# Weight folds on ScalarE, and a new pair's first chunk ahead of the last conv chunk

## The chip, the core and the metric

The kernel runs on one core of a Trainium2 chip. Its metric is the time of one execution in microseconds (us). The core's engines work through their own instruction queues, each in the order in which the program was written: TensorE (PE, matrix products), VectorE (DVE), ScalarE (ACT, activation functions), GpSimd (POOL) and SyncE (SP, which here issues the loads and stores). They meet through semaphores.

## What is computed

The input is 16 images of 192 channels and 56x56 positions in float32. Three layers of a bidirectional RWKV recurrence are followed by a graph convolution. Each has a group normalization in front and adds its result to its input. Cut to what matters:

```
def layer(x):                                  # three times
    xs = tokens(group_norm(x))                 # 3136 tokens of 192 channels
    k, v, r = xs @ Wk.T, xs @ Wv.T, xs @ Wr.T
    w = -exp(w_decay)
    x_bi = 0.5 * (wkv_scan(w, u, k, v) + flip(wkv_scan(w, u, flip(k), flip(v))))
    h = layer_norm(sigmoid(r) * x_bi)
    return x + (h @ Wo.T)

def conv(x):                                   # once, at the end
    g = group_norm(x)
    m = max(roll(g, 2, H), roll(g, -2, H), roll(g, 2, W), roll(g, -2, W)) - g
    y = batch_norm(conv_w @ concat(g, max(m, 0)) + conv_b)
    return x + gelu(y)
```

`wkv_scan` is a weighted running average over the tokens: a numerator p and a denominator q decay by the factor exp(w) per token, and the current token enters with a bonus exp(u).

## The kernel before

Two images form a pair, so that 2 x 192 channels fill three groups of 128 partitions. There are 8 pairs. The 3136 tokens are cut into 7 chunks of 448. A forward unit of a layer, called A, does one chunk in rising order: the key product (`a_keys`) and its exponential (`a_exp`), the value product (`a_values`), exp(k) times v (`a_ekv`), the scans of q and p (`a_q`, `a_p`, line 850), the bonus on each (`a_den`, `a_num`, line 865), the inverse of q as exp(-ln q) on ACT (`invert`), and the quotient on POOL (`a_y`). The scan's last column is copied into the next chunk's tile: `a_save` (ACT) for q, and line 861 within `a_p` for p. A backward unit, B, does one chunk in falling order: the gate product (`b_gate`, `b_exp`, `b_sigmoid`), the scans and bonuses (`b_q`, `b_p`, `b_den`, `b_num`), `b_mix` on POOL (nine operations, lines 991 to 993), and then a tail in stages: squares (ACT) and sums (PE), `b_rs1` to `b_rs3` for the deviation, `b_spread` (PE, tile `rsb`) and `b_scale` (DVE), `b_out` (PE), and `b_x` (DVE, called by `add`), which adds to x. `sum_up` calls `b_stats`, which counts sums and sums of squares of the new x on ACT (lines 724 and 725, tile `fjunk`). A conv unit, C, does two products per chunk (`c_product`), the maxima (`c_rows`, `c_columns`, lines 1075 to 1091, on DVE), and `c_end` with Gelu on ACT and an addition on POOL (L1118). `z_stats` counts the statistics of a later pair's input, one chunk (Z) at a time, on ACT, at the end of a step.

The normalization isn't applied to x: `norm_sums`, `norm_var` and `norm_fold` turn the statistics into a factor per channel, refine it by one Newton step (lines 765 to 768), and multiply the weights of keys and values by it (`fold`, lines 758 to 760, tile `wkv`). For the conv layer line 771 first subtracts one half of the weights from the other. `norm_fold_r` does the gate weights on POOL. These four parts stand in a list, and each call of `gap()` executes one; `begin_now` executes what is left when a unit needs its weights.

The order of all work is written out by hand. A list of 249 steps is made first; a step holds at most one B unit of one pair and one A or C unit of another. There are two streams, the even and the odd pairs, and while one stream runs a layer backwards the other runs its next layer forwards. Each step is executed by one function:

- `both_a` and `both_a_first` (102 steps): B beside A. 25.0 us in the middle of a layer.
- `both_c` (42 steps): B beside C. About 24 us.
- `backward_alone` (24 steps): the first B chunk of a layer.
- `forward_a` and `forward_c` (66 and 14 steps): a lone chunk.
- `neither` (one step): `finish` does what is left of the tails.

At six places a new pair starts: step 53 has the last backward chunk of the other stream beside C5, step 54 is the lone conv chunk C6, and steps 55 to 61 are the seven chunks of the new pair's first layer, A0 to A6, all alone. The other five places are at steps 69, 116, 131, 178 and 193. At the program's start the first pair's A0 to A6 are alone as well (steps 0 to 6), and at its end the last pair's seven conv chunks (steps 242 to 248). The dictionary `late` holds the tails that aren't done, by stage: 0 (nothing yet), 0.5 (`b_rs1` done), 1 (deviation done), 2 (product done, to be added). In `forward_a` and `forward_c` the tail's parts stand between the parts of the chunk, and the parts for the next chunk's keys (`keys`, `exp_keys`) too.

Loads are issued on SP by `load_ahead`, stores by `store` and `b_x`; tiles come from a list of 33 slots and 7 PSUM banks.

Of the kernel before, what the change touches and what calls it, by code (L numbers as in the profile page):

```python
# [40 lines left out]
C = 192  # L41
# [432 lines left out]
def fast_path(ctx: ExitStack, tc: tile.TileContext, flag, x, wproj, wfold, wcfold, wconst, wgroup, sums, picks, vecs, out):  # L474
# [280 lines left out]
        V.tensor_copy(s.full[:, :, L : L + 1], run.nm)  # L755

    def fold(eng, w, rstd):
        eng.tensor_scalar(w[:, :, 0:C], w[:, :, 0:C], rstd[:, 0, :], None, ALU.mult)
        eng.tensor_scalar(w[:, :, C : 2 * C], w[:, :, C : 2 * C], rstd[:, 2, :], None, ALU.mult)
        eng.tensor_scalar(w[:, :, 2 * C : FCOLS], w[:, :, 2 * C : FCOLS], rstd[:, 1, :], None, ALU.mult)  # L760

    def norm_fold(run):
        rstd, t = run.rstd, stile("gt")

        V.tensor_mul(t, rstd, rstd)
        V.tensor_mul(t, t, run.var)
        V.tensor_scalar(t, t, -0.5, 1.5, ALU.mult, ALU.add)
        V.tensor_mul(rstd, rstd, t)
        w, wr = run.weights
        if run.l == NLAYERS:  # L770
            V.tensor_sub(w[:, 0, :], w[:, 0, :], w[:, 1, :])
        fold(V, w, rstd)
        run.w = [folded(w[:, 0, :]), folded(w[:, 1, :])]
        if run.l < NLAYERS:
            run.new = new_stats()
        run.begun = True
# [20 lines left out]
        load_ahead(("C" if run.l == NLAYERS else "A", run, 0))  # L797
        norms.extend((part, run) for part in (norm_sums, norm_var, norm_fold, norm_fold_r))

    def gap():  # L800
        if norms:
            part, run = norms.pop(0)
            part(run)

    def begin_now(run):
        while not run.begun:
# [358 lines left out]
    while ready[turn] is not None:  # L1165
        run, other = ready[turn], 1 - turn
        units = []
        ready[other] = None
        while todo[other]:
            r = todo[other].pop(0)  # L1170
            units += front(r)
            if r.l < NLAYERS:
                ready[other] = r
                break
        steps.append([("B", run, NL - 1), None, None])
        for c in reversed(range(NL - 1)):
            steps.append([("B", run, c), units.pop(0) if units else None, None])
        steps += [[None, u, None] for u in units]
        if len(streams) == 1 or ready[other] is None:

            units = []
            while todo[turn]:
                r = todo[turn].pop(0)
                units += front(r)
                if r.l < NLAYERS:
                    ready[turn] = r
                    break
            else:
# [18 lines left out]
    def of_stage(n):  # L1207
        return next((u for u, stage in late.items() if stage == n), None)

    def sum_up():  # L1210
        while unsummed:
            b_stats(*unsummed.pop(0))

    def squares_and_sums(u):
        b_squares(*u)
        b_sums(*u)
# [32 lines left out]
    def both_a(b, a, nback, nfront):  # L1249

        den = lambda: a[0].den[a[1]]
        l = of_stage(0.5)
        load_ahead(nback)
        load_ahead(nfront)
        store()
        if nback is not None:
            b_gate(*nback[1:])
            b_exp(*nback[1:])
        b_q(*b)
        if l:  # L1260
            b_rs2(*l)
            b_rs3(*l)
        b_sigmoid(*b)
        a_values(*a)
        if l:
            b_spread(*l)
        b_p(*b)
        b_den(*b)
        invert(b[0].ek[b[1]])
        b_num(*b)  # L1270
        b_mix(*b)
        if l:
# [12 lines left out]
        b_squares(*b, (2,))  # L1285
        exp_keys(nfront, (1,))
        b_squares(*b, (1,))
        b_sums(*b)
        a_p(*a)
        gap()  # L1290
        a_den(*a)
        b_rs1(*b)
        late[b] = 0.5
        invert(den())
        gap()
        a_num(*a)
        a_y(*a)
        gap()
# [45 lines left out]
    def both_c(b, a, nback, nfront):  # L1344

        l0, l1, l2 = of_stage(0), of_stage(1), of_stage(2)
        load_ahead(nback)
        load_ahead(nfront)
        store()
        b_q(*b)  # L1350
        b_p(*b)
        if l0:
            squares_and_sums(l0)
        b_den(*b)
        ln(b[0].ek[b[1]])
        if l0:
            b_rs1(*l0)
        exp_minus(b[0].ek[b[1]])
        if l2:
            add(l2)  # L1360
            sum_up()
        if l1:
            spread_and_scale(l1)
        gap()
        if nback is not None:
            b_gate(*nback[1:])
            b_exp(*nback[1:])
        c_product(*a, 0)
        c_rows(*a)
        c_columns(*a)  # L1370
        c_product(*a, 1)
        gap()
        if l0:
            b_rs2(*l0)
            b_rs3(*l0)
            late[l0] = 1
        gap()
        b_num(*b)
        b_sigmoid(*b)
        b_mix(*b)  # L1380
        if l1:
            add(l1)
            sum_up()
        if nback is not None:
            b_q(*nback[1:])
            b_p(*nback[1:])
        if l0:
            spread_and_scale(l0)
        c_end(*a, False)
        keys(nfront)  # L1390
        exp_keys(nfront)
        late[b] = 0

    def forward_a(a, nback, nfront):
        l = next(iter(late), None)
        den = lambda: a[0].den[a[1]]
        a_values(*a)
        load_ahead(nback)
        ahead = nfront is not None and nfront[1].begun
        if ahead:  # L1400
            load_ahead(nfront)
        if l and late[l] == 2:
            add(l)
            l = None
        if l and late[l] == 0:
            squares_and_sums(l)
            b_rs1(*l)
            late[l] = 0.5
        if not l and ahead:
            keys(nfront)  # L1410
        store()
        a_q(*a)
        a_save(*a)
        if l:
            if late[l] == 0.5:
                b_rs2(*l)
                b_rs3(*l)
            b_spread(*l)
            a_den(*a)
            invert(den())  # L1420
            sum_up()
            a_ekv(*a)
            b_scale(*l)
            b_out(*l)
            if nback is not None:
                b_gate(*nback[1:])
            if ahead:
                keys(nfront)
                exp_keys(nfront)
            a_p(*a)  # L1430
            a_num(*a)
            add(l)
            sum_up()
            gap()
        else:
            if ahead:
                exp_keys(nfront)
            a_den(*a)
            gap()
            invert(den())  # L1440
            a_ekv(*a)
            gap()
            sum_up()
            if nback is not None:
                b_gate(*nback[1:])
            a_p(*a)
            gap()
            a_num(*a)
        a_y(*a)
        if nback is not None:  # L1450
            b_exp(*nback[1:])
        if not ahead:
            load_ahead(nfront)
            keys(nfront)
            exp_keys(nfront)

    def forward_c(a, nback, nfront):
        l0, l1, l2 = of_stage(0), of_stage(1), of_stage(2)
        h = of_stage(0.5)
        if h:  # L1460
            b_rs2(*h)
            b_rs3(*h)
            l1 = h
        load_ahead(nback)
        ahead = nfront is not None and nfront[1].begun
        if ahead:
            load_ahead(nfront)
            keys(nfront)
            exp_keys(nfront)
        if l1:  # L1470
            spread_and_scale(l1)
            l2 = l1
        if l0:
            b_squares(*l0)
        c_rows(*a)
        if l2:
            add(l2)
        c_columns(*a)
        c_product(*a, 0)
        store()  # L1480
        if l0:
            b_sums(*l0)
            b_rs1(*l0)
        c_product(*a, 1)
        if l0:
            b_rs2(*l0)
            b_rs3(*l0)
            late[l0] = 1
        c_end(*a, nfront is not None and nfront[0] == "C" and not l0)
        if not ahead:  # L1490
            sum_up()
        gap()
        gap()
        gap()
        if not ahead:
            load_ahead(nfront)
            keys(nfront)
            exp_keys(nfront)
# [15 lines left out]
    def backward_alone(b, nback, nfront):  # L1514
# [5 lines left out]
        gap()  # L1520
        b_den(*b)
        invert(b[0].ek[b[1]])
        b_sigmoid(*b)
        b_p(*b)
        b_num(*b)
        b_mix(*b)
        gap()
        for u in list(late):
            finish(u)
        if nback is not None:  # L1530
# [155 lines left out]
```

## Time and profile before

| What | Value |
|---|---|
| Median of 3 runs | 5385.69 us (5383.85 to 5390.39) |
| The profiled execution | 5381.18 us, span 5379.3 us |
| Granted TensorE clock | 0.917 |
| Instructions | 50906 |
| DVE busy | 5004.0 us, 93% |
| PE busy | 4618.0 us, 86% |
| ACT busy | 3634.0 us, 68% |
| POOL busy | 2784.1 us, 52% |
| DMA, mean | 90 GB/s |

The span is the time from the profile's first to its last instruction; the profiled execution's own time is 1.9 us longer. Busy shares are averages over stages of different kinds, so the places that the change touches are read in the timeline, where a line gives the start, the duration, the engine, the source line, the operation with its output and inputs, how many such instructions follow each other, and in brackets how long the engine had been idle before and what released it. Instructions of one engine overlap by about 0.08 us when the second doesn't wait for the first.

### The profile page before, as it was taken

The page shows a single profiled execution, that of the slowest core. Times are in us where ns is not written, and L with a number is a line of the kernel's source. Part 1 is how long each engine was busy: PE and PEld are TensorE (multiplying, and loading weights), DVE is VectorE, ACT ScalarE, POOL GpSimd, SP SyncE. Part 2 cuts the span into 40 slices and gives each one's busy share as a digit, 9 for nine tenths or more (in the row PEclk, how much of TensorE's full clock was granted, in tenths as well). Part 3 has the DMA queues.
Part 4 walks back from the last instruction along what each step waited for, and adds up shares of the span by engine and source line. Part 5 has one row for each costly group of instructions (what it writes and reads, how often), then busy time and mean ns, then how long its engine had stood idle before and what let it go on. Part 6 is the DMA issues. An engine that isn't in the chain of part 4 may idle for free. (4 is left out here: it accounts for less than half of the span.)

```text
span 5379.3 us, 50906 instructions
## 1 busy us (share of the span) xinstructions
PE 4618.0 (86%) x15206; PEld 1484.1 (28%) x15206; DVE 5004.0 (93%) x6628; ACT 3634.0 (68%) x6891; POOL 2784.1 (52%) x2164
## 2 busy tenths in 40 slices
PE   6788888989798888898879888888888888898897
PEld 2222222223232222222323222222222222222222
DVE  6899999998999999999898999999989899999996
ACT  6677767766676776676676767667767566766773
POOL 1456555654454565565444456555535455555563
PEclk8889989989899998999989999999998999999998
DMA  5222212134242222213425121221343312122233
GB/s 149 77 75 77 85 69 85 66 102 140 73 136 77 86 68 72 74 67 118 138 81 148 57 74 67 85 74 62 118 131 95 110 57 71 66 85 78 79 98 118
DMA packets 314270, 482.41 MB, mean 90 GB/s; under 512 B 66432, under 2 KB 306688, under 8 KB 313984
## 3 DMA queue, kind: packets, MB, share of 16 engines
q1 hardware_dynamic: 312832, 477.59, 27.8%
q8 instruction: 123, 2.02, 0.2%
q10 hardware_dynamic: 1152, 1.48, 0.1%
q14 instruction: 163, 1.34, 0.1%
HBM read 324.83 MB, written 154.14 MB: 89 GB/s over the span
## 5 line engine op out<-in xcount | busy, mean ns | idle before, releaser
L850 DVE TENSOR_TENSOR_SCAN q<-fdecays,ek 128x449 f32<-128x449 f32 (+1 forms) x1008 | 1024.3, 1070 | 23.8 <-POOL p L935 15.6
L991 POOL TENSOR_TENSOR ekv<-ekv,ek 128x448 f32<-128x448 f32 x504 | 614.2, 1219 | 808.0 <-ACT rs L1025 224.8
L850 DVE TENSOR_TENSOR_SCAN p<-fdecays,ekv 128x449 f32<-128x449 f32 (+1 forms) x1008 | 1024.0, 1071 | 5.0 <-POOL p L935 1.8
L935 POOL TENSOR_TENSOR p<-p,q 128x1344 f32<-128x1344 f32 x168 | 511.7, 3046 | 774.6 <-ACT q L931 387.9
L993 POOL TENSOR_TENSOR p<-p,sg 128x448 f32<-128x448 f32 x504 | 596.5, 1183 | 50.3 <-ACT sg L931 7.6
L992 POOL TENSOR_TENSOR p<-p,ekv 128x448 f32<-128x448 f32 x504 | 600.0, 1190 | 39.5
L861 POOL COPY ekv<-p 128x3 f32<-128x3 f32 x271 | 215.1, 794 | 726.9 <-DVE p L850 564.5
L885 ACT ACTIVATE ek<-k,k 128x448 f32<-128x448 f32 x504 | 292.8, 631 | 306.5 <-PE k L595 275.9
L1000 ACT ACTIVATE ek<-p 128x448 f32<-128x448 f32 x504 | 280.9, 573 | 228.2 <-POOL p L993 227.4
L725 ACT ACTIVATE fjunk<-x 128x448 f32<-128x448 f32 x672 | 387.6, 577 | 56.3 <-issue 24.0
L865 DVE SCALAR_TENSOR_TENSOR q<-ek,fcc,q 128x896 f32<-128x896 f32 x336 | 388.4, 1196 | 35.8 <-ACT ek L859 29.9
L1031 PE MATMUL rsb<-rs,fpicks 32*128 32x448 f32 (+1 forms) x1008 | 349.2, 609 | 74.1 <-ACT rs L1025 74.1
L592 PE MATMUL ops<-p,fwo 128*128 128x448 f32 x336 | 225.7, 762 | 203.9 <-DVE p L1036 203.5
L724 ACT ACTIVATE fjunk<-x 128x448 f32<-128x448 f32 x600 | 343.2, 572 | 12.9
L1049 DVE SCALAR_TENSOR_TENSOR x<-ops,fwob,x 128x448 f32<-128x448 f32 x504 | 317.0, 673 | 33.9 <-PE ops L601 23.4
L865 DVE SCALAR_TENSOR_TENSOR ek<-ek,fcc,q 128x896 f32<-128x896 f32 x336 | 343.6, 1063 | 3.1 <-POOL chk L941 3.1
L903 DVE SCALAR_TENSOR_TENSOR ekv<-v,v,ek 128x448 f32<-128x448 f32 x504 | 313.5, 676 | 8.3 <-PE v L601 4.4
L956 ACT ACTIVATE sg<-r,r 128x448 f32<-128x448 f32 x504 | 312.4, 626 | 7.7 <-PE r L595 3.8
L865 DVE SCALAR_TENSOR_TENSOR p<-ekv,fcc,p 128x896 f32<-128x896 f32 x336 | 297.7, 927 | 16.3 <-POOL ekv L861 15.7
L1036 DVE TENSOR_TENSOR p<-p,rsb 128x448 f32<-128x448 f32 x504 | 281.3, 613 | 32.2 <-PE rsb L1031 32.2
L865 DVE SCALAR_TENSOR_TENSOR ekv<-ekv,fcc,p 128x896 f32<-128x896 f32 x336 | 297.7, 927 | 1.2
L928 ACT ACTIVATE ek<-ek 128x1344 f32<-128x1344 f32 x168 | 221.6, 1319 | 86.6 <-DVE ek L865 86.6
(232 smaller groups left out, 11541.2 us busy)
## 6 DMA issues: line engine op xcount, KB each, us to landing
x<-xd SPq DMA_DIRECT2D x240, 672.0 KB, 5.7
xd<-x SPq DMA_DIRECT2D x168, 672.0 KB, 3.9
x<-in_x_dram SPq DMA_DIRECT2D x320, 224.0 KB, 4.5
x<-in_x_dram SPq DMA_DIRECT2D x320, 112.0 KB, 4.4
out_dram<-ml SPq DMA_DIRECT2D x112, 224.0 KB, 2.3
ring<-xd SPq DMA_DIRECT2D x112, 168.0 KB, 5.4
wkv<-in_wfold_dram SPq DMA_DIRECT2D x24, 640.0 KB, 5.4
out_dram<-ml SPq DMA_DIRECT2D x112, 112.0 KB, 2.3
```

Source lines behind the costliest of these rows:

```text
L724: S.activation(junk, xt[:, j, :], AF.Identity, accum_out=stats[:, 0, j, c : c + 1])
L725: S.activation(junk, xt[:, j, :], AF.Square, accum_out=stats[:, 1, j, c : c + 1])
L850: V.tensor_tensor_scan(out, dec[:, column(j)].to_broadcast([P, L if first else L + 1]), e, 0.0, ALU.mult, ALU.add)
L865: by_channel(lambda js, i: V.scalar_tensor_tensor(dst.t[:, js, :], e.t[:, js, :], cc[:, i : i + 1], state.t[:, js, :], ALU.mult, ALU.add))
L903: V.scalar_tensor_tensor(e.t[:, j, :], ps[j][:, 0:L], b[:, j, :], run.ek[c].t[:, j, :], ALU.add, ALU.mult)
L935: G.tensor_mul(run.h[c].t, run.h[c].t, den.t)
L956: S.activation(sg.t[:, j, :], ps[j][:, 0:L], AF.Exp, bias=b[:, j, :], scale=-1.0, accum_out=run.chk[:, at : at + 1])
L991: G.tensor_mul(y.t[:, j, :], y.t[:, j, :], den.t[:, j, :])
L992: G.tensor_add(h.t[:, j, :], h.t[:, j, :], y.t[:, j, :])
L993: G.tensor_mul(h.t[:, j, :], h.t[:, j, :], sg.t[:, j, :])
L1031: PE.matmul(ps[j][:, :L], pick[rows, j, :], rs[rows, :], start=True, stop=True)
L1049: V.scalar_tensor_tensor(xj, ps[j][:, 0:L], wob[:, column(j)], xj, ALU.add, ALU.add, accum_out=run.new[:, 0, j, c : c + 1] if c == 0 else ...
```

## The change

Four things change.

1. `fold` can run on ACT, as an activation Identity with the factor as scale, and the fold of the key and value weights, and of the conv's, always does. The Newton step runs on the engine that `gap` is given, VectorE by default. `backward_alone` calls `gap(G)`, G being POOL, before the sigmoid, and no longer has a gap behind `b_mix`.
2. In the list of steps, the new pair's A0 changes places with the other pair's last conv chunk C6 in the six places. As the loads for the new pair begin two steps ahead of A0, its normalization moves from step 53 to step 52. `both_c` does the next chunk's keys ahead of the conv products where no B unit follows.
3. `forward_a` without a tail under way: the values' product with exp(k) and the scan of p come ahead of both bonuses; p's last column is saved by ACT, here and in `both_a`; a tail of stage 2 is added behind `a_save`, and one of stage 0 gets its squares, sums and `b_rs1` behind `a_p`; one gap instead of three; `sum_up(1)` counts at most one chunk.
4. `forward_c` handles a tail of stage 0.5 alone, and one product stands ahead of the maxima.

```diff
     def fold(eng, w, rstd):
-        eng.tensor_scalar(w[:, :, 0:C], w[:, :, 0:C], rstd[:, 0, :], None, ALU.mult)
...
+        for cols, j in ((slice(0, C), 0), (slice(C, 2 * C), 2), (slice(2 * C, FCOLS), 1)):
+            if eng is S:
+                S.activation(w[:, :, cols], w[:, :, cols], AF.Identity, scale=rstd[:, j, :])
+            else:
+                eng.tensor_scalar(w[:, :, cols], w[:, :, cols], rstd[:, j, :], None, ALU.mult)
...
-    def norm_fold(run):
+    def norm_fold(run, eng):
...
-        V.tensor_mul(t, rstd, rstd)
...
+        eng.tensor_mul(t, rstd, rstd)
+        eng.tensor_mul(t, t, run.var)
+        eng.tensor_scalar(t, t, -0.5, 1.5, ALU.mult, ALU.add)
+        eng.tensor_mul(rstd, rstd, t)
...
-            V.tensor_sub(w[:, 0, :], w[:, 0, :], w[:, 1, :])
-        fold(V, w, rstd)
+            eng.tensor_sub(w[:, 0, :], w[:, 0, :], w[:, 1, :])
+        fold(S, w, rstd)
...
+        if len(units) > NL:
+
+            units[NL - 1], units[NL] = units[NL], units[NL - 1]
...
-        a_p(*a)
+        a_p(*a, S)
...
     def both_c(b, a, nback, nfront):
...
             b_exp(*nback[1:])
+        else:
+            keys(nfront)
+            exp_keys(nfront)
         c_product(*a, 0)
...
-        keys(nfront)
-        exp_keys(nfront)
         late[b] = 0
 
     def forward_a(a, nback, nfront):
-        l = next(iter(late), None)
+        l = of_stage(0.5) or of_stage(1)
+        l0, l2 = of_stage(0), of_stage(2)
...
         else:
+            if l2:
+                add(l2)
+            if ahead:
+                keys(nfront)
+            a_ekv(*a)
             if ahead:
                 exp_keys(nfront)
+            a_p(*a, S)
+            if l0:
+                squares_and_sums(l0)
+                b_rs1(*l0)
+                late[l0] = 0.5
             a_den(*a)
+            invert(den())
+            a_num(*a)
             gap()
-            invert(den())
-            a_ekv(*a)
-            gap()
-            sum_up()
+            sum_up(1)
             if nback is not None:
                 b_gate(*nback[1:])
-            a_p(*a)
-            gap()
-            a_num(*a)
         a_y(*a)
...
     def forward_c(a, nback, nfront):
-        l0, l1, l2 = of_stage(0), of_stage(1), of_stage(2)
         h = of_stage(0.5)
...
+        c_product(*a, 0)
+        c_rows(*a)
+        if h:
+            b_rs2(*h)
+            b_rs3(*h)
+        c_columns(*a)
+        store()
+        if h:
+            b_spread(*h)
+            b_scale(*h)
+        if ahead:
             keys(nfront)
             exp_keys(nfront)
...
         c_product(*a, 1)
-        if l0:
-            b_rs2(*l0)
-            b_rs3(*l0)
-            late[l0] = 1
-        c_end(*a, nfront is not None and nfront[0] == "C" and not l0)
+        if h:
+            b_out(*h)
+            late[h] = 2
+        c_end(*a, nfront is not None and nfront[0] == "C")
...
     def backward_alone(b, nback, nfront):
...
         invert(b[0].ek[b[1]])
+        gap(G)
         b_sigmoid(*b)
...
         b_mix(*b)
-        gap()
```

More of the change, by code (lines that the diff above doesn't have):

```diff
@@ L757, in fold @@
     def fold(eng, w, rstd):
-        eng.tensor_scalar(w[:, :, 0:C], w[:, :, 0:C], rstd[:, 0, :], None, ALU.mult)
-        eng.tensor_scalar(w[:, :, C : 2 * C], w[:, :, C : 2 * C], rstd[:, 2, :], None, ALU.mult)
-        eng.tensor_scalar(w[:, :, 2 * C : FCOLS], w[:, :, 2 * C : FCOLS], rstd[:, 1, :], None, ALU.mult)
-    def norm_fold(run):
-        rstd, t = run.rstd, stile("gt")
[L765 to L769, printed above, removed]
+        for cols, j in ((slice(0, C), 0), (slice(C, 2 * C), 2), (slice(2 * C, FCOLS), 1)):
[4 more added lines that the diff above has]
+    def norm_fold(run, eng):
+        rstd, t = run.rstd, stile("gt")
+        eng.tensor_mul(t, rstd, rstd)
+        eng.tensor_mul(t, t, run.var)
+        eng.tensor_scalar(t, t, -0.5, 1.5, ALU.mult, ALU.add)
+        eng.tensor_mul(rstd, rstd, t)
+        w = run.weights[0]
         if run.l == NLAYERS:
-            V.tensor_sub(w[:, 0, :], w[:, 0, :], w[:, 1, :])
-        fold(V, w, rstd)
+            eng.tensor_sub(w[:, 0, :], w[:, 0, :], w[:, 1, :])
+        fold(S, w, rstd)
         run.w = [folded(w[:, 0, :]), folded(w[:, 1, :])]
@@ L798, in begin_later, with gap @@
         norms.extend((part, run) for part in (norm_sums, norm_var, norm_fold, norm_fold_r))
-    def gap():
+    def gap(eng=V):
         if norms:
             part, run = norms.pop(0)
-            part(run)
+            if part is norm_fold:
+                part(run, eng)
+            else:
+                part(run)
     def begin_now(run):
@@ L1208, in of_stage, with sum_up @@
         return next((u for u, stage in late.items() if stage == n), None)
-    def sum_up():
-        while unsummed:
+    def sum_up(most=NL):
+        for _ in range(min(most, len(unsummed))):
             b_stats(*unsummed.pop(0))
@@ L1367, in both_c @@
             b_exp(*nback[1:])
+        else:
+            keys(nfront)
+            exp_keys(nfront)
         c_product(*a, 0)
@@ L1401, in forward_a @@
             load_ahead(nfront)
[L1402 to L1410, printed above, removed]
         store()
@@ L1457, in forward_c @@
     def forward_c(a, nback, nfront):
-        l0, l1, l2 = of_stage(0), of_stage(1), of_stage(2)
         h = of_stage(0.5)
[L1460 to L1463, printed above, removed]
         load_ahead(nback)
@@ L1467, in forward_c @@
             load_ahead(nfront)
+        c_product(*a, 0)
[9 more added lines that the diff above has]
+        if ahead:
             keys(nfront)
             exp_keys(nfront)
-        if l1:
-            spread_and_scale(l1)
-            l2 = l1
-        if l0:
[L1474 to L1483, printed above, removed]
-        c_product(*a, 1)
-        if l0:
-            b_rs2(*l0)
-            b_rs3(*l0)
-            late[l0] = 1
-        c_end(*a, nfront is not None and nfront[0] == "C" and not l0)
+        c_product(*a, 1)
+        if h:
+            b_out(*h)
+            late[h] = 2
+        c_end(*a, nfront is not None and nfront[0] == "C")
         if not ahead:
             sum_up()
-        gap()
-        gap()
-        gap()
-        if not ahead:
+            gap()
+            gap()
+            gap()
             load_ahead(nfront)
@@ L1526, in backward_alone @@
         b_mix(*b)
-        gap()
         for u in list(late):
```

## The prediction

> **What bounds the kernel now.** I read the page first: VectorE (DVE) is busy 93% of the span, so almost everywhere a chunk lasts as long as its DVE work. Then I read the timeline by engine at the three kinds of place that the change touches.
>
> ```profile
> PE 4618.0 (86%) x15206; PEld 1484.1 (28%) x15206; DVE 5004.0 (93%) x6628; ACT 3634.0 (68%) x6891; POOL 2784.1 (52%) x2164
> ```
>
> *Layer boundary* (step 23, `backward_alone`). The timeline shows DVE doing Newton and fold with no idle time, then TensorE (PE) starting the next layer's keys, and ScalarE (ACT) waiting for them:
>
> ```profile
> 560.63 1.10 DVE L765 TENSOR_TENSOR gt<-rstd 128x3 f32<-128x3 f32 x1
> ...
> 561.97 0.99 DVE L767 TENSOR_SCALAR gt<-gt 128x3 f32<-128x3 f32 x1
> ...
> 563.19 1.18 DVE L758 TENSOR_SCALAR wkv<-wkv,rstd 128x384 f32<-128x384 f32 x1
> 564.29 1.28 DVE L759 TENSOR_SCALAR wkv<-wkv,rstd 128x384 f32<-128x384 f32 x1
> 565.49 1.36 DVE L760 TENSOR_SCALAR wkv<-wkv,rstd 128x512 f32<-128x512 f32 x1
> ...
> 564.62 1.84 PE L592 MATMUL k<-x,wkv 128*128 128x449 f32 x2 [6.73 <-DVE wkv L758]
> ...
> 569.31 0.23 ACT L835 ACTIVATE k<-k 128x1 f32<-128x1 f32 x2 [6.00 <-PE k L595]
> ```
>
> *Lone chunks at a new pair's start* (steps 54 to 57). Here DVE is stretched by POOL (step 54) and idles (steps 55, 56):
>
> ```profile
> 1293.96 4.30 DVE L1090 TENSOR_TENSOR ml<-ml,x 128x1344 f32<-128x1344 f32 x1
> 1298.29 1.56 DVE L1091 TENSOR_TENSOR m<-m,ml 128x1344 f32<-128x1344 f32 x1
> ...
> 1306.81 3.26 DVE L865 SCALAR_TENSOR_TENSOR q<-ek,fcc,q 128x896 f32<-128x896 f32 x2 [2.84 <-ACT ek L859]
> ...
> 1326.08 0.20 DVE L730 TENSOR_REDUCE mv<-stats 128x6 f32<-128x42 f32 x1 [5.64 <-ACT fjunk L725]
> ...
> 1341.07 0.16 DVE L765 TENSOR_TENSOR gt<-rstd 128x3 f32<-128x3 f32 x1 [4.82 <-ACT rstd L748]
> ...
> 1347.06 1.75 DVE L865 SCALAR_TENSOR_TENSOR p<-ekv,fcc,p 128x896 f32<-128x896 f32 x2 [0.34 <-POOL ekv L861]
> ```
>
> *A steady lone chunk* (step 57, by windows: length, PE, PEld, DVE, ACT, POOL busy): ACT and PE have room, DVE has 0.6 us of idle.
>
> ```profile
> 1348.70:1360.60 11.90, 8.83 (x24) 2.78 (x22) 11.27 (x15) 8.30 (x18) 3.22 (x2) 0.86 0.02 5
> ```
>
> **What the Trainium skill says.** "SBUF — State Buffer", section "SBUF: two separate sides": VectorE and GpSimd hold a shared port pair as an exclusive lock for a whole instruction, VectorE when it reads two SBUF tensors or runs in a 2-port mode. The trace agrees: L1090 took 4.30 us beside a POOL add of 3.07, its equal L1091 1.56 alone. "TensorE: Matmul & The Clock Gate", section "Part 1: The HAM clock gate": TensorE runs at half rate after an idle window. The trace agrees in kind: the keys product after 6.73 us idle takes 6.5 us, the values product behind it 4.6.
>
> **Part 1: Newton and fold at boundaries.** Newton (L765 to L768) and fold (L758 to L760) occur 32 times; 17 lie in `backward_alone` at the gap that becomes `gap(G)`, and only there does Newton go to POOL. DVE loses 6.22 us there in 12 cases (560.63 to 566.85), 4.72 in step 15, and 7.88 in the four before a conv layer (with L771).
>
> The fold's price on ACT: no row has 384 or 512 columns. From 0.57 us at 448 and 1.33 at 1344 (0.84 ns a column): 0.52+0.52+0.63 = 1.67 us. "ScalarE: Activation LUTs", section "What ACT_TABLE_LOAD costs", gives 279+0.833N ns with one pointer operand, 93 overlapping: an estimate of 1.63. I take 1.67. Newton on POOL: like L941, 0.20 each, 0.8 in all; blocked by `b_den` at most 2.5. `rstd` is ready at 554.67, POOL is idle until 559.14, and ACT reaches the fold at 558.90, behind `invert`: hidden; without that cover it would cost its 0.8 to 2.5. Behind the fold, ACT's sigmoid comes 1.67 later, at 563.1, when POOL's first L993 wants it (563.01): nothing. POOL's `b_p` save stays behind Newton, unharmed.
>
> What is late next: keys start at 559.45, not 564.62, so 5.2 earlier. DVE could come 6.1 earlier, but values, gate and sums (4.6+4.6+1.7 on PE) set the `b_rs2` of step 24. I take 5.2; bounds 4 and 6.1. **12 x 5.2 = 62.** Step 15: ACT ends `invert` at 372.79, keys start at 373.4, not 375.70: 2.2. Step 7 (`begin_now`, Newton stays): 3.2. Conv boundaries: in step 48 PE runs without a gap from sums (waiting for POOL's mix, end 1144.63) to `rsb` at 1162.25, and DVE took that without waiting; DVE 7.9 earlier only waits. 0.7 x 4 = 3 (bounds 0, 8). First and last fold, uncontended on DVE (0.4 each): 0.5 lost.
>
> **Part 2: steady lone chunks.** `a_ekv` now stands behind `a_q`, and `a_den` between `a_p` and `a_num`, so the waits for the saves (0.28 and 0.34, each against a normal overlap of 0.08) vanish: 0.73 a chunk. 29 such chunks, and 7 last ones at 0.35: **24 gained.** ACT's chain per chunk (save 0.2, key exps 1.7, save 0.2, `invert` 2.7, counted stats 4.2) is 9.0 of 11.1: it follows. In `both_a` the save on ACT in place of POOL's copy (1.03, waiting behind DVE) changes nothing: neither waits for what counts; bounds -3 and 3 over all.
>
> **Part 3: six pair starts.** The order becomes A0, C6, A1. Norm parts move to step 52 (+1.9 on DVE: sums 0.2, variance 1.0, Newton 0.7; the fold there is ACT's, and holds the sigmoid, which POOL's mix awaits), keys of A0 to step 53, squares and sums of the last backward chunk from C6 to A0. POOL's fold of the gate weights (3.3) moves ahead of step 53's mix, beside `c_columns`; DVE has about 5 us to spare there before `rsb`. The stretching falls: in step 54 it is 7.8 us (L1076 0.93, L1077 0.94, three L1088 2.85, L1090 2.74, L1087 0.38 over their lone times), and beside the moved C6 POOL has one `a_y` of 3.0 instead of the mix. But the work becomes one chain, by the durations of the same rows before (a product 4.58, sums 1.7, `rsb` 1.97, three scans 3.05). From step 52's mix, which ends 2.5 late, so that step 53's sums start at 1270.0 and not 1267.45: sums 1.7, keys 4.6, conv 9.1, first `rsb` 1.1, `b_scale` to 1288.1; out and values to 1296.5; ekv 2.2, p 3.0 to 1301.7; save, squares, sums, `b_rs1` to 1304.9; `invert` to 1307.6; stats of B and of Z, 4.2 each, to 1316.1, ahead of `b_rs3` (1.3) on ACT; `rsb` 2.0, keys 4.6 to 1324.0; conv, out, values 13.8 to 1337.8; ekv, p, den, num to 1345.1. PE idles 8 us before the keys, so up to 2 for its slow rate: 1346 against 1348.7. The norm parts, now in the next three chunks, cost DVE 2.1 to 2.9 (sums 0.35, variance 1.0, Newton 0.7, for a conv layer L771 0.8): **nothing gained**, bounds -5 and +8 each. The last pair has no Z stats: 4 gained. SP: C6's chunk and ring load one step later, the A1 chunk behind the out store, still 15 us ahead of use: nothing.
>
> **Part 4: the end.** `forward_c` no longer takes a unit of stage 0, so step 240 does none of it and `neither` runs squares, sums, deviation, spread, out, stats in a row: the last add moves from 5285.0 to about 5295: **10 lost** (7 to 13).
>
> Sum: 62+2+3+3-0.5+24+4-10 = 88 from the profiled 5381.2 (span 5379.3), 5293. The median, 5385.7, is 4.5 above: **5297**. The three runs shown differ by 6.5; 0.2% (10.8 us) is about what a measurement of this kernel can tell from no change.
>
> **Rivals.** *A, slower: pair starts on a slow PE.* The ten products of the chain at 6.5 in place of 4.6 cost 19 a start, 114: 5411. It decides from 16 a start. For: PEclk falls where PE gaps come (0.86 in the window above). Against: at the boundary the slow rate lasted for the first 3 us alone (the values product behind the keys took 4.6), and in the chain only three products follow a gap. *B: the fold waits on ACT.* If `invert` or Newton end later, a boundary gives 2.2, as step 15: 12 x 3 less, 5333. For: step 15. Against: 4.2 us of cover elsewhere. *C: pair starts are DVE-bound after all.* Of the 86.5 us of steps 53 to 56, idle 13.5, stretching 7.8 and norm parts 7.3 go, and 4.7 of the last return elsewhere: 24 a start. Half of it gives 5225. Against: the ACT chain. *D: it doesn't do what it says*, Newton staying on DVE: the built order shows POOL at 17 places, so excluded there.
>
> **How the numbers follow.** My forecast 0.60, B 0.15, C 0.15, A 0.07 (all slower), something that cancels it 0.03. Faster 0.90, same 0.03, slower 0.07. The forecast with its bounds spans 5255 to 5335; B and half of C bring the range to 5238 to 5348.
>
> **What would show it.** Right: DVE busy some 130 lower, L758 to L760 on ACT near 0.6; step 24's keys 5 earlier; lone chunks of 11.1; ACT `rs` L1024 of C6 behind `fjunk`; the last conv chunk's stretch gone; the end longer by 10. Wrong: boundaries under 3 or pair starts beyond +8 or -5 us.

## The result, and the profile after

The change takes 5328.27 us (median of 4 runs, 5325.6 to 5330.99) against 5384.77 us (4 runs) on the same chip: a ratio of 0.9893, with a 95% interval of 0.9876 to 0.991. That is 56.5 us faster where 88 had been forecast, and inside the range given (5238 to 5348). The profiled execution took 5330.99 us with a span of 5329.2 us, 50.1 us below the span before. Line numbers in the changed kernel are 5 higher from the scans on (the scans are line 855, `a_ekv` 908, `b_x` 1054); Newton is lines 767 to 770, the fold 760.

The first part of the page, busy time by engine, of the changed kernel:

```profile
PE 4607.2 (86%) x15206; PEld 1484.5 (28%) x15206; DVE 4891.2 (92%) x6460; ACT 3701.4 (69%) x7114; POOL 2750.7 (52%) x2109
```

DVE has lost 112.8 us of work, but the span only 50.1: more than half of the DVE time that was saved has become waiting.

**The layer boundary** (steps 23 and 24), as the timeline of the changed kernel shows it:

```profile
555.57 0.20 POOL L770 TENSOR_TENSOR rstd<-rstd,gt 128x3 f32<-128x3 f32 x1
...
557.84 1.72 ACT L760 ACTIVATE wkv<-wkv,rstd 128x384 f32<-128x384 f32 x3
...
558.03 1.72 DVE L870 SCALAR_TENSOR_TENSOR ekv<-ekv,fcc,p 128x896 f32<-128x896 f32 x2
...
558.49 1.02 PE L592 MATMUL k<-x,wkv 128*128 128x449 f32 x2 [1.56 <-ACT wkv L760]
559.34 0.92 PE L593 MATMUL k<-x,wkv 128*128 128x449 f32 x2
...
559.67 3.05 DVE L855 TENSOR_TENSOR_SCAN q<-fdecays,ek 128x449 f32<-128x449 f32 x3
```

Newton runs on POOL and ends 2.1 us before ACT reaches the fold; the three fold instructions (x3) take 1.72 us; DVE goes from the last bonus into the next chunk's scan without a gap. PE now waits 1.56 us, not 6.73, and its first two pairs of key products take 1.02 and 0.92 us where they took 1.84 and 1.70.

**A lone chunk behind a new pair's start** (step 58), from the timelines of PE and DVE:

```profile
1336.62 0.19 DVE L730 TENSOR_REDUCE mv<-stats 128x6 f32<-128x42 f32 x1
...
1336.95 0.56 PE L606 MATMUL psg<-mv,fgmat 128*128 128x2 f32 x2 [4.79 <-DVE req L633]
...
1337.15 3.06 DVE L855 TENSOR_TENSOR_SCAN q<-fdecays,ek 128x449 f32<-128x449 f32 x3
...
1339.46 1.86 PE L592 MATMUL v<-x,wkv 128*128 128x448 f32 x2
1341.11 1.70 PE L593 MATMUL v<-x,wkv 128*128 128x448 f32 x2
...
1344.08 1.28 DVE L908 SCALAR_TENSOR_TENSOR ekv<-v,v,ek 128x448 f32<-128x448 f32 x2 [3.86 <-PE v L595]
```

This is a wait that the prediction did not have. `norm_sums` writes `mv` on DVE and then small products `psg` on PE. In PE's queue they stand ahead of the next chunk's values; in DVE's queue the new order put `mv` at the chunk's very end. So PE stood still for 4.79 us, started the values late and slowly, and DVE waited for them. By windows (length, then PE, PEld, DVE, ACT, POOL busy with counts, clock, DMA share, GB/s), that chunk beside a steady lone chunk (step 60) and step 241 at the end:

```profile
1337.15:1353.81 16.66, 16.66 (x52) 7.20 (x52) 12.06 (x19) 9.04 (x20) 3.03 (x1) 0.81 0.39 115
1366.20:1377.19 10.99, 7.00 (x22) 1.89 (x20) 10.99 (x14) 8.96 (x22) 2.99 (x1) 1.00 0.21 63
5205.00:5242.52 37.52, 22.48 (x64) 7.75 (x64) 9.01 (x28) 14.09 (x31) 3.02 (x1) 0.68 0.21 68
```

The steady chunk takes 10.99 us, all of it DVE work, against 11.8 to 11.9 before, as forecast. Step 241 is 37.5 us in which DVE works for 9.

**The sum by place.** The start of a step is taken as the start of its first DVE instruction; lengths of steps in the two traces are compared group by group:

| Place | Forecast gain, us | Measured gain, us |
|---|---|---|
| 12 A boundaries (two steps each) | 62 | 66.2 |
| Step 15 with 16 | 2.2 | 2.5 |
| 4 conv boundaries (two steps each) | 3 | 6.5 |
| Steps 0 to 6 (with the first fold) | 3.5 | 4.7 |
| Steps 7 to 13 | 3.2 | -4.7 |
| 6 pair starts, from the last two backward chunks to A1 | 4 | 11.0 |
| The four lone chunks behind each | 17.5 | -23.1 |
| The last lone chunk of each | 2.1 | 2.3 |
| The two steps behind it | 0 | -8.5 |
| The end, step 239 on | -10 | -16.2 |
| Last lone chunks of other layers, all else | 0 | 9.3 |
| Sum | 87.5 | 50.0 |

The forecast set the gain of a pair start's chain against the norm parts in the lone chunks, so the rows of the pair starts and of the four lone chunks are to be read together: 21.5 forecast to be gained, 12.1 measured as lost. In the traces 37.5 us of the forecast gain are missing, by the medians 31.5.

### The profile page after: what moved, and what is told of

Read it like the earlier page. It is cut to its first block, busy times and chain, and to the rows that moved or that the text cites. A ratio compares the mean times of both kernels' runs of the same rounds, so it can differ in the third digit from the quotient of the medians.

```text
span 5329.2 us, 51050 instructions
## 1 busy us (share of the span) xinstructions
PE 4607.2 (86%) x15206; PEld 1484.5 (28%) x15206; DVE 4891.2 (92%) x6460; ACT 3701.4 (69%) x7114; POOL 2750.7 (52%) x2109
## 4 chain that ended last, share of the span: by engine, by line
DVE 52%; PE 28%; ACT 7%; POOL 6%; issue 5%; DMA 2%; SPq 0%; DVEq 0%; POOLq 0%; ACTq 0%
DVE p L855 13%; DVE q L855 10%; DVE q L870 5%; DVE ek L870 4%; DVE ekv L908 3%; DVE p L1041 3%; DVE p L870 3%; DVE ekv L870 3%; DVE x L1054 2%; PE ops L592 2%; PE st L1014 2%; PE ops L594 2%; PE ops L593 2%; PE rsb L1036 2%; POOL p L998 2%
## 5 line engine op out<-in xcount | busy, mean ns | idle before, releaser
L998 POOL TENSOR_TENSOR p<-p,sg 128x448 f32<-128x448 f32 x504 | 610.7, 1212 | 64.2 <-ACT sg L936 17.3
L1036 PE MATMUL rsb<-rs,fpicks 32*128 32x448 f32 (+1 forms) x1008 | 369.2, 644 | 127.4 <-ACT rs L1030 127.4
L870 DVE SCALAR_TENSOR_TENSOR ek<-ek,fcc,q 128x896 f32<-128x896 f32 x336 | 359.4, 1111 | 9.2 <-POOL chk L946 9.2
L870 DVE SCALAR_TENSOR_TENSOR ekv<-ekv,fcc,p 128x896 f32<-128x896 f32 x336 | 320.7, 996 | 1.2
L1123 POOL TENSOR_TENSOR ml<-ml,x 128x1344 f32<-128x1344 f32 x56 | 178.5, 3187 | 221.5 <-ACT ml L1117 221.5
L933 ACT ACTIVATE q<-q 128x1344 f32<-128x1344 f32 x168 | 223.0, 1327 | 98.1 <-DVE q L870 85.3
```

Source lines behind the costliest of these rows:

```text
L870: by_channel(lambda js, i: V.scalar_tensor_tensor(dst.t[:, js, :], e.t[:, js, :], cc[:, i : i + 1], state.t[:, js, :], ALU.mult, ALU.add))
L998: G.tensor_mul(h.t[:, j, :], h.t[:, j, :], sg.t[:, j, :])
L1036: PE.matmul(ps[j][:, :L], pick[rows, j, :], rs[rows, :], start=True, stop=True)
```

## The experiments

Each was timed beside the kernel before on the same chip, which took 5383.4 us for the first four (part 1 alone, the gap behind `a_ekv`, the last tail, both norm parts in step 7), 5385.6 for the next three and for the four repairs together, and 5386.0 for the other three. Gains and losses are differences of medians; those by place come from the traces.

### Part 1 alone

The kernel before, with `fold`, `norm_fold`, `gap` and `backward_alone` of the changed kernel and nothing else.

> The kernel before with part 1 alone: fold on ACT, the Newton step through gap(G) ahead of b_sigmoid. Theory (the boundaries carry the whole gain, and the rest of the change gives back what it earns): in the two traces twelve boundaries are 5.0 to 6.9 us shorter, the four ahead of a conv layer 1.7, step 15 2.5; that alone is 12 x 5.7 + 7 + 2.5 = 78, so 5307 (5300 to 5315), faster than the whole change. Rival (a good part of the gain at a boundary needs the other edits, such as the save on ACT or the bonuses last): boundaries of 3 to 4 us, 5335 to 5345.

Measured: 5294.93 us, ratio 0.9834 (0.9817 to 0.985). Part 1 alone gains 88.5 us, 32 more than the whole change: all other parts together made the kernel slower. By the same grouping its A boundaries give 65.8 and the conv boundaries 6.1, as in the changed kernel (66.2 and 6.5), so the boundary needs nothing of the other parts. The expectation had left out what lies outside the boundaries: 3.3 us in the last lone chunks of layers and 6.6 spread over the 80 other steps with B beside A. What makes those shorter was not examined.

### The gap behind a_ekv

```diff
             a_ekv(*a)
             if ahead:
                 exp_keys(nfront)
+            gap()
             a_p(*a, S)
...
             a_num(*a)
-            gap()
             sum_up(1)
```

> The changed kernel with one edit: in forward_a's lone chunk the gap stands behind a_ekv instead of behind a_num. Theory (at a pair start the small psg products of norm_sums stand on PE ahead of the next chunk's values and wait for DVE's mv, which the new order put at the chunk's very end; the values then come 4.5 us late): mv comes at a_ekv, the psg products follow the keys without a gap, DVE's wait of 3.86 + 0.59 us in steps 58, 73, 120, 135, 182 and 197 goes: 6 x 4.5 = 27 faster, 5301 (5297 to 5306). Rival 1 (mv waits for the statistics on ACT, so an earlier gap blocks DVE instead): within 6 of 5328. Rival 2 (norm parts cost by their own DVE work): no change, 5328.

Measured: 5299.83 us, ratio 0.9842 (0.9826 to 0.9859); 28 below the changed kernel. The theory holds. The same lines of PE and DVE in this kernel's timeline:

```profile
1330.20 0.18 DVE L730 TENSOR_REDUCE mv<-stats 128x6 f32<-128x42 f32 x1
...
1331.93 0.38 PE L606 MATMUL psg<-mv,fgmat 128*128 128x2 f32 x2
...
1333.36 1.02 PE L592 MATMUL v<-x,wkv 128*128 128x448 f32 x2
...
1339.86 1.84 DVE L908 SCALAR_TENSOR_TENSOR ekv<-v,v,ek 128x448 f32<-128x448 f32 x3
```

`psg` now follows the keys without a gap, the values start 6.1 us earlier, and no line has a wait. Step 58 takes 11.92 us instead of 16.66, and the six such chunks are 4.7 to 5.1 us shorter each.

### The last tail in step 240 again

`forward_c` gets its tail parts back: `b_squares` at the start, `add` of the stage-2 tail behind `c_rows`, `b_sums` and `b_rs1` behind the maxima, `b_rs2` and `b_rs3` ahead of `c_end`.

> The changed kernel, with forward_c doing the last backward chunk's tail again: squares at the start, sums and b_rs1 behind the maxima, b_rs2 and b_rs3 ahead of c_end, and the addition of the stage-2 tail behind c_rows; only step 240 has such tails. Theory (the end of the last backward layer is serial in step 241): steps 240 and 241 took 50.7 us against 36.7 before, so 12 to 14 come back: 5315 (5313 to 5318). Rival (the tail's chain is as long wherever it starts, since ACT's statistics and PE at its slow rate set it): under 5 back, 5324 to 5328.

Measured: 5311.66 us, ratio 0.9865 (0.9849 to 0.9882); 16.6 below the changed kernel. Steps 240 and 241 take 35.0 us, against 50.7 and, before the change, 36.7. In the changed kernel's timeline of ACT the squares come 21.6 us behind the end of POOL's mix (5196.78), behind Gelu and a chunk's statistics:

```profile
5212.23 0.72 ACT L1117 ACTIVATE ml<-cv,cvb,finv 128x448 f32<-128x448 f32 x1 [0.87 <-PE cv L601]
...
5217.77 0.58 ACT L725 ACTIVATE fjunk<-x 128x448 f32<-128x448 f32 x1
5218.35 1.49 ACT L1005 ACTIVATE ek<-p 128x448 f32<-128x448 f32 x3
```

### Both norm parts at gap(G) in step 7

```diff
-        gap(G)
+        while norms and norms[0][0] is not norm_fold_r:
+            gap(G)
```

> The changed kernel, with backward_alone executing every norm part ahead of the first that concerns the gate weights at gap(G); this changes step 7 alone, where Newton and fold then run on POOL and ACT ahead of b_sigmoid, and not behind b_num and POOL's mix. Theory (steps 7 to 10 are a chain from A0's keys over ACT and POOL, and what the keys gain stays): keys 4 to 6 us earlier, and still 4 to 6 us in step 14: 5323. Rival (steps 8 to 13 are set by the input loads, the Z statistics on ACT and the out product on a slow PE): the lead of step 8 is gone by step 14, 5326 to 5329.

Measured: 5327.24 us, ratio 0.9894 (0.9878 to 0.9911): no difference in the times. In the trace steps 7 to 13 are 3.3 us shorter (196.9 against 200.2 us), 2.4 of it in step 7, and it stays in step 14. That lies between the two expectations.

Where the gain of these steps went, the traces of three kernels tell. With part 1 alone step 7 is 5.4 us shorter than before, and steps 8 to 13 are 5.4 longer, so the fold's gain is lost behind step 7 whatever the lone chunks do; no run gives the reason. In the changed kernel step 7 is only 0.9 shorter, and steps 8 to 13 are 5.6 longer. The difference in step 7 is a wait that both of its forms have. DVE's timeline, first before, then in the changed kernel:

```profile
148.26 0.17 DVE L730 TENSOR_REDUCE mv<-stats 128x6 f32<-128x42 f32 x1
```

```profile
147.84 0.20 DVE L730 TENSOR_REDUCE mv<-stats 128x6 f32<-128x42 f32 x1 [4.36 <-ACT fjunk L725]
```

DVE enters step 7 4.9 us earlier than before, and waits 4.4 for statistics that ACT ends at 147.7, almost as late as before (147.9). With the bonuses last, `a_den` of the last chunk ends at 138.9, before at 139.0; `invert` and the statistics behind it on ACT gained nothing from the shorter chunks. No run moved `a_den` back, so this cause is read from the traces and not tested.

### b_rs3 ahead of the statistics

```diff
             a_num(*a)
+            if l0:
+                b_rs2(*l0)
+                b_rs3(*l0)
+                late[l0] = 1
             gap()
```
(and `forward_c` takes the tail of stage 1)

> The changed kernel with one move: b_rs2 and b_rs3 of the last backward chunk stand in A0's step behind a_num, ahead of the statistics of B and Z, instead of in C6's step. Theory (at a pair start 8.4 us of statistics on ACT stand ahead of b_rs3, and rsb, the keys of A1, the conv product, the out product and the values follow in one chain): b_rs3 ends near 1287 instead of 1295, b_scale is bound by DVE's maxima (3.5 us earlier), the keys' exponentials by the statistics, the A1 values 8 to 10 us earlier; 5 starts of 8 to 10 and the last pair's, without Z statistics, of 4: 5328 - 48 = 5280 (5275 to 5295). Rival (PE at its slow rate and POOL's work set these steps): under 10 in all, 5318 to 5328.

Measured: 5307.37 us, ratio 0.9855 (0.9838 to 0.9871): 21 below the changed kernel, less than half of what was expected. In the changed kernel's timeline the chain is there (ACT, PE, DVE in C6's step):

```profile
1293.91 0.66 ACT L1029 ACTIVATE rs<-rs,feps 64x448 f32<-64x448 f32 x1
...
1295.23 3.72 PE L1036 MATMUL rsb<-rs,fpicks 32*128 32x448 f32 x6 [8.39 <-ACT rs L1030]
...
1303.98 3.06 DVE L855 TENSOR_TENSOR_SCAN q<-fdecays,ek 128x449 f32<-128x449 f32 x3 [4.03 <-ACT ek L890]
```

`b_rs3` now ends at 1287.4, as expected, and C6's step takes 15.36 us, not 22.55; A0's step gets 2.2 longer, because DVE there waits 1.4 us for ACT's part of `b_rs1` and then does `b_rs2` (0.6). But PE in this kernel's timeline shows the next wait:

```profile
1289.37 1.02 PE L592 MATMUL k<-x,wkv 128*128 128x448 f32 x2
1295.04 1.86 PE L593 MATMUL k<-x,wkv 128*128 128x448 f32 x2 [4.65 <-DVE p L1041]
```

After one block of the keys, PE waits 4.65 us for DVE's `b_scale`, which reads `rsb` and frees its PSUM bank, and which stands behind 8 us of maxima. By the kernel's text the conv product holds three of the 7 banks and `rsb` three, which leaves one for the keys. As long as `rsb` came late, that place had cost nothing.

### Newton on DVE

```diff
-        gap(G)
+        gap()
```

> The changed kernel with gap() in place of gap(G) in backward_alone at the same place, so that the Newton step stays on DVE there (0.7 us, 17 places; 0.8 more for the conv layer's subtraction at four of them) and the fold stays on ACT. Theory (at a boundary DVE has no idle time behind it in the changed kernel, -2.2 us in step 24, so its work counts in full at the twelve A boundaries): 12 x 0.7 = 8 slower, 5336; the conv boundaries, where DVE waits 2.9 us in the next step, nothing. Rival (the products of the next step set its end, as the prediction said): 5328.

Measured: 5342.9 us, ratio 0.9917 (0.99 to 0.9933): 14.6 slower. The A boundaries lose 12.8 us in the trace. Ten of the twelve lose 0.2 to 1.4 each, mostly 0.5, where 0.7 had been expected for the bare DVE work. PE waits for the folded weights as long as in the changed kernel (1.55 us for 1.56 ahead of step 24), so it is DVE's work that counts there. The other two (steps 23 with 24 and 39 with 40) lose 3.8 and 3.6. In step 24 a later product, `ops`, ran at PE's slow rate, behind two gaps of 1.03 and 0.94 us on PE, and DVE waited 3.3 us for it; step 40 looks alike. The lines of step 24, first with Newton on DVE, then in the changed kernel:

```profile
583.45 1.86 PE L592 MATMUL ops<-p,fwo 128*128 128x448 f32 x2 [0.94 <-DVE p L1041]
```

```profile
581.37 1.02 PE L592 MATMUL ops<-p,fwo 128*128 128x448 f32 x2
```

So the traces put most of the loss of these two down to a slow PE and not to Newton's own time. The conv boundaries lose 2.0 each, and not nothing: there the 0.7 of Newton and the 0.8 of the subtraction do lie on the path. So Newton's place was worth 14.6 us, about a sixth of what part 1 gains alone, and the fold is left with the rest.

### The exchange undone

First with the earlier gap, to be compared with the second and third experiments together (the recorded texts call this run the fifth experiment):

```diff
-        if len(units) > NL:
-            units[NL - 1], units[NL] = units[NL], units[NL - 1]
```
(and `forward_c` of the kernel before)

> The changed kernel without the exchange of A0 and C6, with forward_c as before the change (it takes all tails, so the end is as before), and with forward_a's gap behind a_ekv as in the second experiment. Its counterpart with the exchange is the changed kernel with both repairs, about 5300 less 16 = 5283. Theory (the exchange gains about 1 us a start in steps 52 to 57, but puts 2.7 us of norm parts into the lone chunks behind, where DVE has no idle time): without it 6 x 1.8 faster, 5272 (5266 to 5280). Rival (the exchange pays, because C6 loses its stretch by POOL, 7.8 us a start): 5300 to 5330.

Measured: 5248.01 us, ratio 0.9745 (0.9729 to 0.9761). That is the direction of the theory, but 24 us below its number: A1 takes 16.8 us in step 56, where it took 22.2 before the change and 21.7 with the exchange. Then with the gap where the change has it:

> The changed kernel with only the exchange of A0 and C6 undone, and forward_c as before the change (without the exchange the tails reach C6, so this one is needed); forward_a's gap stands where the change put it, behind a_num. Theory (the order C6, A0, A1 is better with the new forward_a than the order A0, C6, A1, and norm_sums then falls into A0's step, where nothing waits for PE at the chunk's end): about as the fifth experiment, 5250 (5242 to 5262), so the exchange with its forward_c costs 75 us beside what the rest of the change brings. Rival (the fifth experiment was fast because of its earlier gap alone): 27 more, 5277, or above.

Measured: 5252.44 us, ratio 0.9755 (0.9739 to 0.9771). This undoes the exchange and the new `forward_c` (points 2 and 4 of the change) and is 76 us faster than the changed kernel. Read with the first experiment: part 1 gains 88 us, this kernel 133, so the new `forward_a` and what comes with it adds 45, where 24 had been forecast for the lone chunks, and the exchange with its `forward_c` takes 76 back. If the second and third experiments may be subtracted, 28 of the 76 are waits like that of step 58 and 17 the end; the other 31 are the exchange itself, 5 a start. Steps 52 to 61 of the two traces (without the exchange and with it, both with the early gap) take 162.1 against 167.0 us: steps 52 and 53, with the norm parts of the new pair, 46.7 against 48.6; C6 and A0 together 42.2 against 39.0; A1 16.8 against 21.7; A2 to A6 56.4 against 57.8. The exchange gains where it was meant to, 3.3 us in C6 and A0, and A1 behind them gives back more.

### Two kernels that go further

With the four repairs together (early gap, last tail, `b_rs3` early, step 7), the exchange kept:

> The changed kernel with four repairs together: the gap behind a_ekv, the last tail in step 240 again, b_rs2 and b_rs3 ahead of the statistics at pair starts, and both norm parts at gap(G) in step 7. Theory (the four act at different places and add up): 27 + 16 + 48 + 3.5 = 94 faster than the changed kernel, 5234 (5225 to 5250). Rival (the move of b_rs3 only brings the next wait forward): 47 faster, 5281.

Measured: 5251.65 us, ratio 0.975 (0.9733 to 0.9766): 77 below the changed kernel; the sum of the four alone is 28 + 17 + 21 + 1 = 67. Where the other 10 come from was not examined. Then with `b_spread` and `b_scale` ahead of `c_columns`, and `b_out` ahead of the second `c_product`:

> The kernel with the four repairs, and in C6's step b_spread and b_scale ahead of the column maxima and b_out ahead of the second conv product. Theory (with b_rs3 early, the keys of A1 wait 4.65 us for a PSUM bank that b_scale on DVE frees, and b_scale stands behind 8 us of maxima): the keys run straight behind rsb, the out product and A1's values come 6 us earlier: 6 x 6 = 36 faster, 5216 (5210 to 5228). Rival (DVE now waits 2 to 3 us for rsb ahead of its maxima, and the second conv product, behind them, holds the values as before): within 10 of 5252.

Measured: 5220.56 us, ratio 0.9693 (0.9677 to 0.9709): 31 more. The keys of A1 now run straight behind `rsb` without their wait, C6's step falls from 15.42 to 12.28 us and A1's from 22.00 to 20.36. That fits the PSUM bank as the next wait; but two things were moved at once, and what `b_out` alone is worth was not measured. A1 still waits 6.45 us for its values, which stand on PE behind the second conv product.

Last, without the exchange and with the early gap, with both norm parts at `gap(G)` in step 7 (1 us by itself) and the norm sums moved out of A0's step:

```diff
             add(l)
             sum_up()
-            gap()
+            if nback is not None:
+                gap()
```

> The fifth experiment's kernel, with both norm parts at gap(G) in step 7, and with forward_a's gap behind a tail left out where a lone chunk follows, so that norm_sums comes in A1's step behind a_ekv and not at the end of A0's. Theory (at the end of step 55 DVE waits 5.65 us for the statistics on ACT, and the psg products behind it put PE's values of A1 4.9 us later, and PE into its slow rate, 7.3 us for the values): a_q of A1 then waits for the keys' exponentials alone, 2.2 us, and the values come straight behind the keys: 9 us a start less 1 to 2 for the norm parts, which now stand in chunks without idle time: 5248 - 3 - 42 = 5203 (5198 to 5222). Rival (the statistics, or the keys of A2 behind them on ACT, set A1's end anyway): under 12 in all, 5236 to 5246.

Measured: 5209.74 us, ratio 0.9672 (0.9655 to 0.9688), the fastest of all, 176 us below the kernel before. DVE's waits around A1 without this edit (first fence, the first kernel of "The exchange undone") and with it (second), from the timelines:

```profile
1299.72 0.20 DVE L730 TENSOR_REDUCE mv<-stats 128x6 f32<-128x42 f32 x1 [5.64 <-ACT fjunk L725]
1307.05 1.27 DVE L908 SCALAR_TENSOR_TENSOR ekv<-v,v,ek 128x448 f32<-128x448 f32 x2 [3.75 <-PE v L595]
```

```profile
1298.12 3.06 DVE L855 TENSOR_TENSOR_SCAN q<-fdecays,ek 128x449 f32<-128x449 f32 x3 [1.82 <-ACT ek L890]
1301.96 1.28 DVE L908 SCALAR_TENSOR_TENSOR ekv<-v,v,ek 128x448 f32<-128x448 f32 x2 [0.78 <-PE v L595]
```

The wait of 5.64 us for the statistics was in the kernel before too; it was shown in the prediction, at 1326.08, and nobody had moved it.

## Why the prediction was right or wrong

**The bound and the boundaries: right.** Step 23 with 24 gave 4.6 where 5.2 was taken; eight of the twelve gave 5.7 to 5.9, because they had been longer before (17.3 us, not 16.6); in step 31, where this was looked up, DVE had waited 0.92 us for `psg`, and 0.24 in step 23, while Newton and fold took the same 6.22. The claim that PE, and not DVE, would limit the following step does not hold: in step 24 DVE works for 29.0 of 29.2 us, and in "Newton on DVE" more work for DVE made such steps longer with the keys where they were. DVE gains 5.5 us in step 23 and loses 0.9 of it in step 24, because the four bonuses now fall beside POOL's mix. In step 24, first before, then in the changed kernel:

```profile
572.69 1.72 DVE L865 SCALAR_TENSOR_TENSOR ek<-ek,fcc,q 128x896 f32<-128x896 f32 x2
574.33 1.74 DVE L865 SCALAR_TENSOR_TENSOR ekv<-ekv,fcc,p 128x896 f32<-128x896 f32 x2
```

```profile
565.59 2.61 DVE L870 SCALAR_TENSOR_TENSOR ek<-ek,fcc,q 128x896 f32<-128x896 f32 x2
568.12 3.51 DVE L870 SCALAR_TENSOR_TENSOR ekv<-ekv,fcc,p 128x896 f32<-128x896 f32 x2
```

So that 5.2 came near to what was measured is luck as far as PE was its reason. The keys took 4.6 us with a wait of 1.56 us ahead of them, where they had taken 6.5. "TensorE: Matmul & The Clock Gate", section "Part 1: The HAM clock gate", of the Trainium skill says that an idle window halves the rate; the trace agrees, and here the slow rate went with the wait, which the forecast had not counted as a gain. The fold's price (1.67 forecast, 1.72 measured) and Newton's cover on POOL held. The conv boundaries gave 1.6 each where 0.7 was taken, within the bounds 0 to 8.

**The steady lone chunk: right in size.** It gave 0.8 us; the forecast took 0.73, though its own terms add up to 0.78.

**Pair starts: the term that failed.** "The norm parts, now in the next three chunks, cost DVE 2.1 to 2.9": as DVE work they do (11.92 and 12.40 us in the second experiment against 10.99 for a chunk without them, 2.3 together). What was left out is what `norm_sums` puts on PE's queue: the small `psg` products, ahead of the next values and waiting for a reduction at the end of DVE's chunk. That cost 4.7 to 5.1 us at six places, 29 us in all, and it is the largest part of the 37.5 us that are missing. The plan of that chain over PE, ACT and DVE to the start of step 57 was close: forecast 2.7 us ahead of the kernel before, measured 1.4 us, with `b_rs3` behind the statistics as written down. The two steps behind the lone chunks lost another 8.5 us in all, of which the second experiment gave back 3.7. Of the 8.5, 6.5 lie in the first of the two steps, where DVE's `a_den` now waits 1.5 us for POOL's `chk`, 0.4 before (step 62); no run tried to remove that wait. In all a start fell short of the sum by 5.6 us (33.6 over six), just outside the 5 of the bound. The rival that PE's slow rate rules the pair starts had the sign, at a third of its 19 us, and it has a share: the slow rate came with the wait, and the second experiment removed both together. An estimate from the two timelines of step 58: at full rate `psg` and the first two blocks of values would have taken 3.0 us less (1.4 for 2.5, and 2.7 for 4.6), which is most of the 3.86 that DVE waited. What set it off is the wait for `mv`, which the rival did not name.

**The end: right in kind, 16.2 for 10,** outside its bounds of 7 to 13. The tail became serial as forecast. It starts later than assumed, because ACT does Gelu and a chunk's statistics ahead of the squares, and most of its products, from the conv product to the out product, run on a slow PE (clock 0.68 in the window).

**Steps 0 to 13: wrong.** The gain in the first seven chunks came (4.7), but the 3.2 forecast for step 7 did not. In step 7 `mv` waits for ACT, whose statistics start behind `invert`, and the new order had left `a_den`, which `invert` needs, at the end of the chunk: that wait uses up the lead. What step 7 gains by the fold is lost in steps 8 to 13, with part 1 alone too, and this cause stays open.

**The number: partly luck.** The measured time lies within the forecast's own bounds (5255 to 5335), but near their slow edge. The rows that fell short did so by about 56 us, and about 19 came back from rows that gave more than was put down for them: the boundaries of both kinds, and 9.3 us in steps that were put at nothing. Part 1 alone gained 88.5, where its terms in the prediction add up to 70.

**Rivals.** None came as a whole. The rival that the boundary gives 2.2 where ACT is late did not occur. That pair starts are bound by DVE was wrong: DVE waits 26 us in steps 53 to 56 of the changed kernel (4.8, 3.3, 9.9, 8.4); before it was 17.5, not the 13.5 of the prediction. And shortening such waits gained 21 us (early `b_rs3`), 31 (`b_scale` with `b_out`) and 38 (late norm sums, with the edit of step 7 that gave 1 by itself).

## What to carry to other kernels

When a piece of work is moved within one engine's queue, look at what it issues on the other engines' queues and at what stands behind it there: a reduction of 0.2 us at a chunk's end held back a product of 4.6. Time each part of a change alone: here one part was worth 88 us and the others together took 32 of it back, which the total of 56 hides; and among the others, one was worth 45 and another cost 76. And a repaired wait is worth only the distance to the next one; at one place the early `b_rs3` showed the wait for `b_scale`, and its removal the one for the second conv product, each only when the one before was gone.

## What was not expected of the hardware

The rate of PE after a short wait is not a matter of that wait's length alone. In the first kernel of "The exchange undone" the first six `psg` products ran at full rate behind 2.92 us of idle time (0.36 us a pair), the later ones and the values behind them at the slow one (0.56 us a pair, 7.28 us for the values in place of 4.58). With Newton on DVE a product ran slowly behind gaps of 1.03 and 0.94 us in step 24, while in the changed kernel the keys behind 1.56 us at the boundary ran at full rate. And the fold of 1280 columns cost 1.72 us on ACT, where DVE had taken 3.66 beside POOL's mix and 1.15 alone (step 241 before).
